# GpSimd's share of the state products, and the places of three background steps, in a kernel of two convolution layers around scans

## The chip, the cores and the metric

The kernel runs on one core of one Trainium2 chip. The metric is the time of one execution on the device in microseconds (us), lower is better; each time is that of the core, as the device reports it. The engines are named as in the profile: PE is the matmul engine (PEld its weight loads), DVE is VectorE, ACT is ScalarE, POOL is GpSimd, SP is the engine whose queue starts the transfers. They run side by side, each takes its own instructions strictly in order, and they wait for each other on semaphores.

## What is computed

The input is 8 images of 64 channels and 128 by 128 pixels, in float32. Layer 0 is a filter whose 9 taps differ from pixel to pixel; layer 1 holds two blocks of a two-way state scan (a "mamba"), between norms and convolutions. Cut to what matters here:

```python
# layer 0: per pixel 9 weights, from two convolutions and a softmax
w_hp = delta - softmax(conv1x1(leaky(conv3x3(x))))
x1 = x + sum(shifted(x, k) * w_hp[:, k] for k in range(9))
# layer 1
x_norm = layernorm(x1)                 # first norm; also feeds the branch dw1
seq = res = layernorm(x_norm)          # second norm
for l in range(2):                     # two blocks
    xz = in_proj(rmsnorm(seq))         # third norm, for block 0
    seq = seq + out_proj(scan_forward(xz) + scan_backward(xz))
# one scan, for each channel d of 128 and state n of 16, along 16384 pixels:
#   h[t] = exp(dt[t] * A[d, n]) * h[t-1] + dt[t] * u[t] * B[n, t]
#   y[t] = sum over n of h[t] * C[n, t]  + D[d] * u[t], then times silu(z)
x2 = x1 + dwconv(dw1(x_norm)) * (conv3x3(rmsnorm(seq)) + res)     # "mix"
out = x2 + ffn(layernorm(x2))          # convolutions, gelu, gate
```

## The kernel before

The whole program is one list of steps. `at(time, phase, fn)` puts a function at a time (a whole number) and at one of seven phases within it, in the order FEED, SCAN, MID, PROD, EXP, DECAY, REST. At the end the list is sorted by time and phase and its functions are called one after the other, so that each engine's queue holds its instructions in just this order. A time has no duration of its own: one unit of it is one scan on VectorE and what was put beside it.

**Scans.** An image has 16,384 pixels, which a pass takes in 16 chunks of T = 1024. A chunk's states (128 channels x 16) are 16 units of 128 partitions x 1024 pixels, two units to a pair. For each image there are four passes (two blocks, two directions): 1 and 3 are "first" passes, which leave their y in DRAM (yf_dram), and 2 and 4 are "second" passes (self.second), which add it in, multiply by the gate and project. So there are 8 x 4 x 16 = 512 chunks and 8192 scans, 1024 of them for an image. For unit u of a chunk that begins at time t0 = b, `Chunk.plan` sets:

- `drive(k)` at b + 2k - 5: bu = dup x bp for a pair, 128x2048 on GpSimd, into one of 4 buffers (L1186).
- `decay(u)` at b + u - 2: w = exp(dt A) on ScalarE, into one of two PSUM tiles (L1194).
- `scan(u)` at b + u on VectorE (L1213 or L1215, by direction). Where the product will be GpSimd's, the scan writes to hs in SBUF, otherwise in place over w.
- `product(u)`: hs x cp, 128x1024, either on VectorE in the same step (L1230) or on GpSimd a step later (L1232, L1234). `on_pool(u)` says which: before the change units 0, 2, 6, 8, 10 and 14 of every chunk, without those a step behind a gelu of the FFN.
- `keep(u)`: ScalarE copies the last state for the next chunk (L1237).
- `collect(k)` at b + 2k + 3 (pairs 0 and 4 a step later): PE sums a pair's products over the states into the one PSUM tile y (L1252). Pairs 0 and 4 first put D u into it (L1245), which needs the tile free.
- `y_out(h)` for the two halves h of a chunk takes y out: on VectorE with the gate in second passes (L1267), on ScalarE as a copy in first passes (L1269), and then `store_y` sends it to DRAM.
- `dtx` makes du for the next chunk, 128x1024 on GpSimd (L1142); `load_hn` loads a chunk's input two chunks ahead.

**Background.** Beside the scans run three other kinds of work. The *front* of the next image (layer 0 and the norms, 16 chunks, one each 24 steps) runs beside the end of pass 3 and most of pass 4; for image 0 half of it runs before the scans (`plan_alone`) and half beside pass 1. The *mix* of an image (16 chunks, one each 13 steps) runs beside the end of its pass 4 and pass 1 of the next image, the *FFN* (16 chunks, one each 24 steps) beside passes 1 to 3 of the next image. For the last image both follow at other paces, and the FFN comes behind the last scan.

In the front, at a chunk's own time a: nine taps, each with `weight(k)` (PE spreads tap k's weights over the channels into the PSUM tile of the tag "bg", L594), `weighted(k)` (VectorE multiplies them with the shifted image, L598) and `gather(k)` (PE adds it into another PSUM tile, L609). The bank "bg" is one buffer: whoever wants it next waits until the last reader is done. The logits, the transposed softmax, and the means and factors of the first and the third norm use it as well. A norm is: a square on ScalarE, `means` (4 small matmuls on PE, L491), `means_out` (ScalarE: Ln, Exp, L497 and L498), `spread` (PE, L504), and a multiplication on VectorE (L629, L661). ScalarE's copies of small tiles, the squares and the images in work take their room from one pool "tmp" of 11 buffers.

Of the kernel before, what the change touches and what calls it, by code (L numbers as in the profile page):

```python
# [21 lines left out]
NCH = HALF // ROWS  # L22
# [14 lines left out]
FEED, SCAN, MID, PROD, EXP, DECAY, REST = range(7)  # L37
# [18 lines left out]
def kernel(ctx: ExitStack, tc: tile.TileContext, a: dict, out: bass.AP):  # L56
# [385 lines left out]
    def tmp(name):  # L442
        return wk.tile([P, N], F32, tag="tmp", name=name, bufs=11)
# [73 lines left out]
    class Front:  # L517
# [131 lines left out]
                )  # L649

        def second_norm(self):
            self.h0, self.sq = self.hc, tmp("sq")
            nc.scalar.activation(self.h0, self.h0, AF.Identity, bias=vec["pe_norm_b"], scale=vec["pe_norm_w"])
            nc.scalar.activation(self.sq, self.h0, AF.Square)

        def store_h(self):
# [11 lines left out]
        def plan(self, a):  # L668
            n1, n2, n3 = self.n1, self.n2, self.n3
            b = a - FRONT_STEP  # L670
            at(b - 5, REST, self.load_xa)
            for i in range(3):
                at(b + 1 + i, REST, self.hidden, i)
            at(b + 5, DECAY, self.hidden_out)
            at(b + 21, REST, self.logits)
            at(b + 23, DECAY, self.less_max)
            at(b + 23, DECAY, self.exps)
            at(b + 25, MID, self.sums)
            at(b + 25, REST, self.softmax)
            for i in range(3):  # L680
                at(b + 26 + 2 * i, DECAY, self.piece, i)
                if i < 2:
                    at(b + 27 + 2 * i, REST, self.less_piece, i)
            at(b + 31, REST, self.turn)
            at(b + 32, DECAY, self.turned)
            at(a + 6, REST, self.load_xb)
            for k in range(9):

                t = a + k + (k >= 3)
                at(t + 11, DECAY, self.weight, k)  # L690
                at(t + 12, MID, self.weighted, k)
                at(t + 13, REST, self.gather, k)
            at(a + 23, DECAY, self.filtered)
            at(a + 23, REST, self.store_x1)
            at(a + 23, REST, self.centered, acc_tile, "x1")
            at(a + 24, DECAY, self.centered_out)
            at(a + 25, REST, lambda: n1.means(bg_tile, self.sq))
            at(a + 26, DECAY, n1.means_out)
            at(a + 27, REST, n1.spread, bg_tile)
            at(a + 29, MID, self.scaled, n1)  # L700
            at(a + 29, DECAY, self.first_norm)
            at(a + 30, REST, self.pointwise)
            at(a + 31, DECAY, self.pointwise_out)
            at(a + 31, REST, self.store_rows, dw_img[self.p], "dwt")
            at(a + 31, REST, self.centered, acc_tile, "xn")
            at(a + 32, DECAY, self.centered_out)
            at(a + 33, REST, lambda: n2.means(acc_tile, self.sq))
            at(a + 34, DECAY, n2.means_out)
            at(a + 35, REST, n2.spread, acc_tile)
            at(a + 37, MID, self.scaled, n2)  # L710
            at(a + 37, DECAY, self.second_norm)
            at(a + 37, REST, self.store_h)
            at(a + 38, REST, lambda: n3.means(bg_tile, self.sq))
            at(a + 39, DECAY, n3.means_out)
            end = a + (49 if self.c < NCH - 1 else 43)
            at(end - 2, REST, n3.spread, bg_tile)
            at(end, MID, self.third_norm)
            at(end, REST, self.store_hn)

        def plan_alone(self, a):  # L720
            n1, n2, n3 = self.n1, self.n2, self.n3
            b = a - FRONT_STEP
            self.alone = True
            one = bg_tile if self.c in (ALONE - 3, ALONE - 1) else mm_tile
            at(b - 5, REST, self.load_xa)
            for i in range(3):
                at(b + 1 + i, REST, self.hidden, i)
            at(b + 5, DECAY, self.hidden_out)
            at(b + 12, REST, self.logits)
            at(b + 14, DECAY, self.less_max)  # L730
            at(b + 14, DECAY, self.exps)
            at(b + 16, MID, self.sums)
            at(b + 16, REST, self.softmax)
            for i in range(3):
                at(b + 17 + 2 * i, DECAY, self.piece, i)
                if i < 2:
                    at(b + 18 + 2 * i, REST, self.less_piece, i)
            at(b + 22, REST, self.turn)
            at(b + 23, DECAY, self.turned)
            at(a + 6, REST, self.load_xb)  # L740
            for k in range(9):

                t = a + k + (k >= 3)
                at(t + 11, DECAY, self.weight, k)
                at(t + 12, MID, self.weighted, k)
                at(t + 13, REST, self.gather, k)
            at(a + 23, REST, self.store_x1)
            at(a + 23, REST, self.centered, one, "x1")
            at(a + 24, DECAY, self.centered_out)
            at(a + 25, REST, lambda: n1.means(one, self.sq))  # L750
            at(a + 26, DECAY, n1.means_out)
            at(a + 27, REST, n1.spread, one)
            at(a + 29, MID, self.scaled, n1)
            at(a + 29, DECAY, self.first_norm)
            bank = y_tile if a + 37 < 3 else acc_tile
            at(a + 30, REST, self.pointwise, bank)
            at(a + 31, DECAY, self.pointwise_out)
            at(a + 31, REST, self.store_rows, dw_img[self.p], "dwt")
            at(a + 31, REST, self.centered, bank, "xn")
            at(a + 32, DECAY, self.centered_out)  # L760
            at(a + 33, REST, lambda: n2.means(bank, self.sq))
            at(a + 34, DECAY, n2.means_out)
            at(a + 35, REST, n2.spread, bank)
            at(a + 37, MID, self.scaled, n2)
            at(a + 37, DECAY, self.second_norm)
            at(a + 37, REST, self.store_h)
            at(a + 38, REST, lambda: n3.means(bg_tile, self.sq))
            at(a + 39, DECAY, n3.means_out)
            end = a + (43 if self.c < ALONE - 1 else 49)
            at(end - 2, REST, n3.spread, bg_tile)  # L770
            at(end, MID, self.third_norm)
            at(end, REST, self.store_hn)
# [12 lines left out]
    class Mix(Front):  # L785
# [40 lines left out]
        def plan(self, a):  # L826
            n1 = self.n1
            for h in range(2):
                at(a - 6 + h, REST, self.load_conv, dw_img[self.p], "dww", h)
                at(a - 4 + h, REST, self.load_conv, xm_img, "xmw", h)  # L830
            at(a - 1, REST, self.load_h)
            for i in range(3):
                at(a + i, REST, self.conv, 0, "dww", i)
                at(a + 3 + i, REST, self.conv, 1, "xmw", i)
            at(a + 3, DECAY, self.branch_out)
            at(a + 2, REST, self.load_x1)
            at(a + 5, REST, self.add_h)
            at(a + 8, MID, self.times)
            at(a + 8, REST, self.plus)
            at(a + 10, REST, self.store_x2)  # L840
            at(a + 10, REST, self.centered, bg_tile, "x1")
            at(a + 11, DECAY, self.centered_out)
            at(a + 12, REST, lambda: n1.means(bg_tile, self.sq))
            at(a + 13, DECAY, n1.means_out)
            at(a + 14, REST, n1.spread, bg_tile)
            at(a + 16, MID, self.scaled, n1)
            at(a + 16, DECAY, self.norm)
            at(a + 16, REST, self.store_rows, xn_img, "hc")

    def plan_mix(b, a, step):  # L850
        at(a - 4, REST, load_weights, 1)
# [176 lines left out]
    class Chunk:  # L1028
# [143 lines left out]
        def on_pool(self, u):  # L1172


            if u % 2 or u % 8 == 4 or self.t0 + u - 1 in gelu_times:
                return False
            return True

        def over_pair(self, what, k):
            j = self.pairs[k][0]  # L1180
# [132 lines left out]
        def plan(self):  # L1313
# [5 lines left out]
                else:  # L1319
                    at(t - 1, REST, fn, *args)  # L1320

            at(b + 3, REST, self.load_hn)
            for h in range(2):
                feed(b + 7 + h, self.conv, h)
                at(b + 7 + h, DECAY, self.conv_out, h)
# [34 lines left out]
            for h in range(2):  # L1360
                if self.second:
                    at(b + 8 * h + 1, REST, self.load_yf, h)
                    at(b + 8 * h + 6, REST, self.add_yf)
                    at(b + 8 * h + 7, REST, self.load_gate, h)
                if self.second:
                    at(b + 8 * h + 11, MID, self.y_out, h)
                else:
                    at(b + 8 * h + 11, DECAY, self.y_out, h)
                    at(b + 8 * h + 12, REST, self.store_y, h)
            if not self.second:  # L1370
                return
            b += U
# [62 lines left out]
```

## Time and profile before

| | |
|---|---|
| time, median of 3 runs | 28,580.81 us (28,557.65 to 28,581.72) |
| the profiled execution | 28,567.34 us |
| its span, first to last instruction | 28,565.6 us |
| from the first to the last scan | 383 us to 28,119 us |
| ScalarE's Exp for the scans (L1194) | 8192 x 1.119 us |
| scans on VectorE (four groups) | 8192 x 2.343 us |
| products on GpSimd (L1232, L1234) | 1515 x 2.409 us, 1445 x 2.374 us |
| taps of the filter on VectorE (L598) | 1152 x 0.673 us |
| transfers | 237 GB/s over the span |

A line of the costliest groups reads: line, engine, operation, what is written and what is read, their shapes, the count, then busy time in us and the mean of one in ns, then the idle time of the engine just ahead of these instructions and who ended most of it. Lines of the timeline begin with start and duration in us, and end with the idle time before and what ended it, in brackets. Lines of the waits give who waited for whom, the total in us, the number of times and the longest. Spans on GpSimd are rough.

### The profile page before, as it was taken

The numbers are of one execution on the slowest core, as the hardware profiler recorded it, in microseconds if no ns is written. First come the engines' busy times: TensorE is split into PE (matmuls) and PEld (weight loads), VectorE is DVE, ScalarE is ACT, GpSimd is POOL, SyncE is SP. The second block draws the span as 40 slices with busy tenths as digits, with TensorE's granted clock in tenths as the row PEclk, the third lists the DMA queues.
The fourth block names the chain that finished last, engine by engine and source line by source line (L and its number), as shares of the span: only waits on it lengthen the run. The fifth ranks groups of instructions, "written<-read, shape, count | busy, mean of one in ns | idle before, by whom it ended". The sixth has DMA issues, their size and how long they took to land. (4 is left out here: it accounts for less than half of the span.)

```text
span 28565.6 us, 310777 instructions
## 1 busy us (share of the span) xinstructions
PE 22791.3 (80%) x97708; PEld 7199.5 (25%) x97708; DVE 27008.8 (95%) x17438; ACT 18796.6 (66%) x29130; POOL 26723.7 (94%) x8092
## 2 busy tenths in 40 slices
PE   7666878878888787887878788787887878878578
PEld 3212322223222232222322222222222222222123
DVE  6999999999999999999999999999999999999997
ACT  4666666666666666666666666666666666666663
POOL 4999999999999999999999999999999999999993
PEclk7778889988899888988889889898898988889789
DMA  5777787777877778777787777777777777777674
GB/s 161 231 241 226 234 258 245 243 227 236 261 246 243 228 235 265 243 240 228 242 256 244 240 230 244 253 246 235 230 251 247 249 229 236 250 245 248 209 256 138
DMA packets 2592494, 6762.73 MB, mean 237 GB/s; under 512 B 431494, under 2 KB 737046, under 8 KB 2589686
## 3 DMA queue, kind: packets, MB, share of 16 engines
q1 hardware_dynamic: 2589958, 6742.69, 73.0%
q8 instruction: 773, 12.66, 0.2%
q14 instruction: 883, 7.23, 0.1%
q10 hardware_dynamic: 880, 0.14, 0.0%
HBM read 5509.49 MB, written 1265.19 MB: 237 GB/s over the span
## 5 line engine op out<-in xcount | busy, mean ns | idle before, releaser
L1186 POOL TENSOR_TENSOR bu<-dup,bp 128x2048 f32<-128x2048 f32 x4096 | 18669.5, 4569 | 30.2 <-DMA hn_dram<-hn 11.4
L1194 ACT ACTIVATE w<-dtp,a_neg 128x1024 f32<-128x1024 f32 x8192 | 9162.7, 1119 | 1498.3 <-DVE hs L1215 661.3
L1230 DVE TENSOR_TENSOR hs<-w,cp 128x1024 f32<-128x1024 f32 x5232 | 6394.1, 1222 | 254.3 <-DMA cp<-bc_dram 72.7
L1215 DVE TENSOR_TENSOR_SCAN w<-w,state,bu 128x1024 f32<-128x1024 f32 x2651 | 6212.2, 2343 | 144.3 <-ACT w L1194 116.8
L1213 DVE TENSOR_TENSOR_SCAN w<-w,state,bu 128x1024 f32<-128x1024 f32 x2581 | 6048.3, 2343 | 136.5 <-ACT w L1194 127.4
L1252 PE MATMUL y<-hs,sel_y 128*32 128x512 f32 x32768 | 4927.9, 681 | 357.4 <-POOL hs L1234 234.8
L1237 ACT COPY state<-w 128x1 f32<-128x1 f32 x5232 | 829.1, 158 | 5461.1 <-DVE hs L1230 5390.7
L1232 POOL TENSOR_TENSOR hs<-hs,cp 128x1024 f32<-128x1024 f32 x1515 | 3649.2, 2409 | 408.9 <-DVE hs L1213 212.3
L1234 POOL TENSOR_TENSOR hs<-hs,cp 128x1024 f32<-128x1024 f32 x1445 | 3430.0, 2374 | 442.3 <-DVE hs L1215 314.6
L1213 DVE TENSOR_TENSOR_SCAN hs<-w,state,bu 128x1024 f32<-128x1024 f32 x1515 | 3550.7, 2344 | 128.0 <-ACT state L1237 76.6
L1215 DVE TENSOR_TENSOR_SCAN hs<-w,state,bu 128x1024 f32<-128x1024 f32 x1445 | 3384.7, 2342 | 105.8 <-ACT state L1237 72.6
L1061 PE MATMUL xp<-hn,wx 128*128 128x512 f32 x4096 | 2353.2, 703 | 908.8 <-ACT xc L1067 397.5
L1245 PE MATMUL y<-xc,dskip 128*64 128x512 f32 x4096 | 1453.6, 796 | 1231.1 <-ACT yv L1269 1083.8
L892 PE MATMUL fp<-fw,bgw 128*128 128x512 f32 (+1 forms) x5760 | 2155.7, 617 | 169.1 <-DMA fw<-xn_dram 162.1
L1103 PE MATMUL dp<-xc,wdt 128*128 128x512 f32 x2048 | 1296.8, 719 | 650.4 <-ACT dt L1110 316.5
L1252 PEld LDWEIGHTS y<-hs,sel_y 128*32 128x32 f32 x32768 | 719.9, 114 | 3866.9 <-issue 2449.9
L68 ACT ACT_TABLE_LOAD x1137 | 1458.8, 1283 | 21.0 <-PEq L1424 0.7
L1067 ACT ACTIVATE xc<-xp,cbias 128x512 f32<-128x512 f32 x1024 | 701.1, 685 | 1156.1 <-PE xp L1061 1152.7
L898 PE MATMUL fp<-fw,bgw 64*128 64x512 f32 (+1 forms) x5760 | 1386.4, 608 | 0.0
L1061 PEld LDWEIGHTS xp<-hn,wx 128*128 128x128 f32 x4096 | 802.2, 214 | 2307.1 <-issue 878.7
L609 PE MATMUL acc<-t,ident 128*128 128x512 f32 x2160 | 1332.1, 705 | 0.7 <-DVE t L598 0.7
L1142 POOL TENSOR_TENSOR du<-dt,xc 128x1024 f32<-128x1024 f32 x512 | 1225.7, 2394 | 42.0 <-ACT dt L1116 42.0
(212 smaller groups left out, 25302.5 us busy)
## 6 DMA issues: line engine op xcount, KB each, us to landing
bp<-bc_dram SPq DMA_DIRECT2D x4096, 256.0 KB, 4.0
dup<-du_dram SPq DMA_DIRECT2D x4096, 256.0 KB, 5.2
dtp<-dt_dram SPq DMA_DIRECT2D x4096, 256.0 KB, 5.1
cp<-bc_dram SPq DMA_DIRECT2D x4096, 256.0 KB, 4.7
hn<-hn_dram SPq DMA_DIRECT2D x1024, 256.5 KB, 4.5
dt_dram<-dt SPq DMA_DIRECT2D x512, 512.0 KB, 2.9
du_dram<-du SPq DMA_DIRECT2D x512, 512.0 KB, 2.6
yf_dram<-yv SPq DMA_DIRECT2D x512, 256.0 KB, 4.3
```

Of the source, the lines that this page charges most:

```text
L68: nc.scalar.preload_act_table_set("natural_log_exp_and_others")
L892: nc.tensor.matmul(o, wpair[:, i, g, m], self.win[h][:, i : i + ROWS, 0:W], start=(i == 0), stop=False)
L1061: nc.tensor.matmul(self.xp[h], wx[:, self.l, self.d, i, :], self.hn2[:, s.start + 2 * i : s.stop + 2 * i], start=(i == 0), stop=(i == 1),)
L1186: nc.gpsimd.tensor_tensor(bu, self.dup[self.pairs[k][1]], self.over_pair("bp", k), ALU.mult)
L1194: nc.scalar.activation(w, self.dtp[gp][:, i, :], AF.Exp, scale=a_neg[:, self.l, self.d, g, j : j + 1])
L1213: nc.vector.tensor_tensor_scan(to, w, bu, s0, ALU.mult, ALU.add)
L1215: nc.vector.tensor_tensor_scan(to[:, ::-1], w[:, ::-1], bu[:, ::-1], s0, ALU.mult, ALU.add)
L1230: nc.vector.tensor_tensor(out, hs, c, ALU.mult)
L1232: nc.gpsimd.tensor_tensor(out, hs, c, ALU.mult)
L1234: nc.gpsimd.tensor_tensor(out[:, ::-1], hs[:, ::-1], c[:, ::-1], ALU.mult)
L1245: nc.tensor.matmul(self.y[C * h : C * h + C, :], dskip[:, self.l, self.d, C * gp : C * gp + C], self.xc[:, s], start=True, stop=False,)
L1252: nc.tensor.matmul(self.y[lo : lo + 32, :], sel_y, hs[:, i, s], start=False, stop=(k % 4 == 3))
```

## The change

It has these parts.

1. `on_pool`: only unit 4 is left out of the even units, and unit 12 in second passes. In first passes GpSimd also makes the product of unit 12, and VectorE no longer does.
2. The front's third norm: its square is taken out of `second_norm` into a function of its own, `third_square`. For chunks 0 to 14 of a front that runs beside scans it is put at a + 46, its mean at a + 47 (before: a + 38) and Ln and Exp at a + 48; the third norm and its store come at a + 55 instead of a + 49. The last chunk and the fronts of `plan_alone` keep their times. The filter's taps, which had a free step ahead of tap 3, now follow each other without one.
3. In first passes `y_out` and `store_y` come one step sooner.
4. The mix's second half (`centered` to the store of xn) comes one step later.
5. `load_hn` of chunk 14 of all 512 comes two steps later.

```diff
@@ second_norm @@
-            self.h0, self.sq = self.hc, tmp("sq")
+            self.h0 = self.hc
             nc.scalar.activation(self.h0, self.h0, AF.Identity, bias=vec["pe_norm_b"], scale=vec["pe_norm_w"])
+
+        def third_square(self):
+            self.sq = tmp("sq")
             nc.scalar.activation(self.sq, self.h0, AF.Square)
@@ Front.plan @@
-                t = a + k + (k >= 3)
+                t = a + k
                 at(t + 11, DECAY, self.weight, k)
                 at(t + 12, MID, self.weighted, k)
                 at(t + 13, REST, self.gather, k)
...
-            at(a + 38, REST, lambda: n3.means(bg_tile, self.sq))
-            at(a + 39, DECAY, n3.means_out)
-            end = a + (49 if self.c < NCH - 1 else 43)
+            late, end = (a + 46, a + 55) if self.c < NCH - 1 else (a + 37, a + 43)
+            at(late, DECAY, self.third_square)
+            at(late + 1, REST, lambda: n3.means(bg_tile, self.sq))
+            at(late + 2, DECAY, n3.means_out)
             at(end - 2, REST, n3.spread, bg_tile)
             at(end, MID, self.third_norm)
             at(end, REST, self.store_hn)
@@ plan_alone @@
+            at(a + 37, DECAY, self.third_square)
@@ Mix.plan @@
-            at(a + 10, REST, self.centered, bg_tile, "x1")
-            at(a + 11, DECAY, self.centered_out)
...
+            at(a + 11, REST, self.centered, bg_tile, "x1")
+            at(a + 12, DECAY, self.centered_out)
...
@@ Chunk.on_pool @@
-            if u % 2 or u % 8 == 4 or self.t0 + u - 1 in gelu_times:
+            if u % 2 or u == 4 or self.t0 + u - 1 in gelu_times:
                 return False
-            return True
+            return u != 12 or not self.second
@@ Chunk.plan @@
-            at(b + 3, REST, self.load_hn)
+            at(b + (5 if self.i == NCH - 2 else 3), REST, self.load_hn)
...
-                    at(b + 8 * h + 11, DECAY, self.y_out, h)
-                    at(b + 8 * h + 12, REST, self.store_y, h)
+                    at(b + 8 * h + 10, DECAY, self.y_out, h)
+                    at(b + 8 * h + 11, REST, self.store_y, h)
```

More of the change, by code (lines that the diff above doesn't have):

```diff
@@ L840, in plan @@
             at(a + 10, REST, self.store_x2)
[L841 to L848 removed]
+            at(a + 11, REST, self.centered, bg_tile, "x1")
+            at(a + 12, DECAY, self.centered_out)
+            at(a + 13, REST, lambda: n1.means(bg_tile, self.sq))
+            at(a + 14, DECAY, n1.means_out)
+            at(a + 15, REST, n1.spread, bg_tile)
+            at(a + 17, MID, self.scaled, n1)
+            at(a + 17, DECAY, self.norm)
+            at(a + 17, REST, self.store_rows, xn_img, "hc")
     def plan_mix(b, a, step):
```

## The prediction

> **What bounds the kernel now.** I read the page first: the shares of the engines and the costliest groups.
>
> ```profile
> PE 22791.3 (80%) x97708; PEld 7199.5 (25%) x97708; DVE 27008.8 (95%) x17438; ACT 18796.6 (66%) x29130; POOL 26723.7 (94%) x8092
> ...
> L1186 POOL TENSOR_TENSOR bu<-dup,bp 128x2048 f32<-128x2048 f32 x4096 | 18669.5, 4569 | 30.2 <-DMA hn_dram<-hn 11.4
> L1230 DVE TENSOR_TENSOR hs<-w,cp 128x1024 f32<-128x1024 f32 x5232 | 6394.1, 1222 | 254.3 <-DMA cp<-bc_dram 72.7
> ```
>
> VectorE and GpSimd stand at 95% and 94%, too close to say which sets the end. So I cut the trace where a pass begins, at the scan of unit 0 of every sixteenth chunk, and asked for the engines' busy time by pass. The first four rows are passes 1 to 4 of image 4; then pass 1 of image 0, pass 3 of image 0, pass 3 of image 7. The columns are the stretch, its length, and busy time with the count of instructions for PE, PEld, DVE, ACT and POOL; then clock and DMA.
>
> ```profile
> 14294.40:15139.70 845.30, 659.75 (x2842) 178.70 (x2840) 802.78 (x461) 559.05 (x840) 844.28 (x252) 0.89 0.78 253
> 15139.70:16000.10 860.40, 757.11 (x3154) 234.92 (x3150) 832.40 (x506) 592.27 (x880) 812.27 (x230) 0.96 0.74 246
> 16000.10:16858.60 858.50, 648.00 (x2750) 201.03 (x2749) 832.90 (x542) 573.16 (x900) 836.30 (x263) 0.84 0.72 228
> 16858.60:17772.60 914.00, 762.36 (x3535) 274.72 (x3533) 869.66 (x609) 624.06 (x1020) 843.36 (x267) 0.90 0.75 242
> 383.20:1257.00 873.80, 640.22 (x2655) 208.47 (x2654) 837.05 (x545) 574.25 (x915) 835.17 (x262) 0.78 0.70 224
> 2091.00:2956.10 865.10, 602.67 (x2536) 182.22 (x2535) 827.57 (x534) 561.41 (x882) 846.85 (x267) 0.80 0.71 225
> 26438.10:27260.60 822.50, 470.19 (x1684) 103.61 (x1682) 784.83 (x428) 516.55 (x748) 820.07 (x237) 0.73 0.62 209
> ```
>
> In pass 1 GpSimd is busy for 844.3 of 845.3 us while VectorE idles 42.5 us: GpSimd sets the time there. In pass 3 it idles 22 us, in pass 2 48 us, in pass 4 71 us. Then I looked at GpSimd's queue inside pass 1.
>
> ```profile
> 14715.90 4.79 POOL L1186 TENSOR_TENSOR bu<-dup,bp 128x2048 f32<-128x2048 f32 x1
> 14720.39 2.61 POOL L1232 TENSOR_TENSOR hs<-hs,cp 128x1024 f32<-128x1024 f32 x1
> 14722.71 4.76 POOL L1186 TENSOR_TENSOR bu<-dup,bp 128x2048 f32<-128x2048 f32 x1
> 14727.19 2.60 POOL L1232 TENSOR_TENSOR hs<-hs,cp 128x1024 f32<-128x1024 f32 x1
> 14729.50 4.76 POOL L1186 TENSOR_TENSOR bu<-dup,bp 128x2048 f32<-128x2048 f32 x1
> ```
>
> The recorded durations overlap: a product that "takes" 2.61 us is followed 2.32 us later. What a back-to-back instruction costs is the distance of starts: 4.49 and 4.48 us for a drive, 2.32 and 2.31 us for a product. One more reading from the timeline: drives and pairs of scans stand in one order, so the lead of GpSimd (end of a drive to the start of the scan that reads it) can be followed. In image 4 its minimum per chunk falls from 6.7 us in chunk 0 of pass 1 to 0.0 in chunk 3, stays at 0 to 0.5 us up to chunk 9 and is back at 7.4 us in chunk 15; pass 3 starts at 7.2 and ends at 10.2 us. So GpSimd has a cushion of some 7 us, and no more. Last, what VectorE waits for in pass 4, and the longest wait but one:
>
> ```profile
> DVE t L598 <- PE wb L594: 21.7, 13, 3.1
> DVE hs L1213 <- ACT state L1237: 7.2, 10, 1.0
> DVE hn L661 <- PE rb L504: 4.8, 5, 1.6
> ```
> ```profile
> 17410.13 0.69 ACT L1067 ACTIVATE xc<-xp,cbias 128x512 f32<-128x512 f32 x1 [2.73 <-PE xp L1061]
> 17410.71 0.26 ACT L497 ACTIVATE r<-ms,eps 128x8 f32<-128x8 f32 x1
> 17411.03 0.38 PE L594 MATMUL wb<-wt,sel_k 65*128 65x512 bf16 x1 [0.94 <-ACT r L497]
> 17411.44 0.69 DVE L598 TENSOR_TENSOR t<-xb,wb 128x512 f32<-128x512 f32 x1 [2.95 <-PE wb L594]
> ```
>
> The third norm's mean and the filter's weights use one PSUM bank. ScalarE must take the mean out (L497), but it stands behind the conv eviction L1067, which waited 2.73 us for PE; then tap 3's weight, and VectorE has waited 2.95 us. Of the 21.7 us, 16.5 us are at tap 3, right behind the mean, and 5.2 us at tap 8.
>
> **Part 1: unit 12 on GpSimd.** Its product leaves VectorE in all 256 chunks of first passes (1 and 3): 256 x 1.222 = 313 us off VectorE, 19.6 us a pass. On GpSimd it costs 16 x 2.31 = 37.0 us a pass, 591 us in all. In the built order the products on GpSimd go from 2960 to 3216. What a pass becomes is GpSimd's busy time before, plus 37.0, corrected for the change in lead:
> - Pass 1, images 1 to 7 (before 844.4 to 846.0 us): 844 + 37 = 881. The lead used to come back to 7 by the end; now it stays at 0, and pass 2, with 48 us of GpSimd idle, restores it: 881 - 7 = 874, so +29, times 7 = +203. Bounds +26 (a lead of 10 drawn down) to +36 (none drawn): 182 to 252.
> - Pass 3, images 1 to 6 (mean 857.3): 836.3 + 37.0 = 873.3, less the 3 by which the lead grew, less 4 as it now falls from 7 to 3 = 866, so +9, times 6 = +54. Bounds +6 (lead to 0) to +37 (the 22 us of idle stays): 36 to 222.
> - Pass 3, image 7: 820.1 + 37.0 against 822.5, lead to 0 in both: +35 (33 to 37).
> - Image 0: pass 1, 835.2 + 37.0 less some 1 for the lead = 871 against 873.8; I take 0 (-3 to 20). Pass 3, 846.9 + 37.0 less 9 of growth plus 2 = 877: +12 (8 to 37).
>
> Sum: 203 + 54 + 35 + 0 + 12 = **+304 us** (256 to 568). The 313 us off VectorE bring nothing where GpSimd is last, and are in the sum already where it isn't.
>
> The Trainium skill, "Perfetto Trace Analysis", section Identifying the Most-Contended Engine, says that the engine with the highest occupancy is the bottleneck, and that it may change between regimes. By its first half over the whole span, VectorE (95%) is to be relieved, and the sum would be -313 for this part and 28,135 us in all; by its second half, read pass by pass, it agrees with the rows.
>
> **Part 2: the mean behind the filter, without the free step at tap 3.** Nothing is added: 1 square, 4 small matmuls, Ln and Exp per chunk of the front, later; the two stores of hn go 6 steps later on SP. It acts where VectorE is last: pass 4, images 0 to 6 (913.9 to 917.2 us). In pass 3 and in image 0's pass 1 the same waits are hidden by GpSimd. The tap-3 wait goes: 16.5 us an image. What is late next: the mean, now at front step 23, stands between the logits' readers and the next chunk's first mean in the same bank, each a step (3.3 to 3.6 us) apart; and tap 8, now a step sooner. I take 17 an image, **-119 us** for seven. Bounds: 0 (as long a wait moves elsewhere) to 27 an image (the rb waits of 4.8 too): 0 to -189. A loss can't be excluded: h0 keeps one of the 11 tmp buffers 6 steps longer.
>
> **Part 3: at nothing.** y_out stands a scan sooner in first passes: PE's wait for yv (PEld y from L1245, 47.6 us in pass 1 of image 4, 89.0 in pass 3) shrinks, but GpSimd hides it. On ScalarE it now stands ahead of unit 13's Exp instead of unit 14's; if PE is late, that Exp is late, and the scan. VectorE's slack of 42.5 + 19.6 us in pass 1 covers this. In pass 3, 25.6 + 19.6 - 9 covers less; gone, it is in the +37 bound. The store of y moves with it, same count. The mix's centered goes a step later: PE waited 46.0 us in pass 1 for POOL's x (PEld cp), hidden by GpSimd. load_hn moves in one chunk of 512 (its two transfers land after 4.5 us, two steps are some 6.6). The tail after the last scan (446 us) keeps its order but for the last mix chunks: 0.
>
> **Sum.** The profiled run took 28,567.3 us (span 28,565.6): 28,567.3 + 304 - 119 = 28,752. The median of the runs is 13.5 us above it, so I forecast **28,765 us**, 0.65% slower.
>
> **Rivals.**
> - The tap-3 wait only changes place (PE at 762 of 914 us in pass 4 is often late, and its queue order decides): 28,765 + 119 = 28,885. For it: the chain begins with PE's xp, which stays. Against: the Ln leaves the chain. 20%.
> - No cushion: the waits that make GpSimd idle in pass 3 stay and each product costs its 2.31 us in full: 28,581 + 591 - 119 = 29,053. For it: a late product on GpSimd holds PE's collect and everything behind. Against: in pass 1 GpSimd idles 1 us with the lead at 0, so lateness of the others doesn't reach it. 7%.
> - More gain: the low end of part 1 and all waits of part 2: 28,581 + 256 - 189 = 28,648. 10%.
> - Faster: GpSimd's records are rough, and its 100% in pass 1 is room that isn't seen; VectorE sets the time everywhere and gets its 313 us back: 28,581 - 313 - 119 = 28,149. It decides if 16 chunks with one product more still fit into 845 us, which needs GpSimd 4.2% quicker per instruction (881/845). For it: VectorE's 95%. Against: starts 2.31 and 4.48 us apart, a lead of 0, and VectorE idle in the same stretch. 3%.
>
> **How the numbers follow.** The forecast's own case has 60%, and reaches from 28,680 to 28,860. The range of 28,630 to 28,930 takes in the first rival and most of the third, and leaves out the second and the last and part of the edges. About 0.2% (57 us) is what a measurement of this kernel can tell from no change. Faster than that 3%, within it 5% (the far end of the third rival), slower 92%.
>
> **What will show it.** Pass 1 of images 1 to 7 near 874 us with GpSimd idle under 3 us, its lead at 0 from chunk 3 or sooner to the end, and VectorE idle up from 42 to some 90 us. Pass 3 near 866 us. Pass 4 near 897 us with hardly a wait of L598's line behind tap 3. Pass 2 unchanged near 860 us. I am wrong if pass 1 stays near 845 us, if pass 2 grows by what is left over from pass 1, or if the filter's wait turns up at another tap.

## The result and the profile after

The changed kernel takes 28,852.8 us (median of 4 runs, 28,841.6 to 28,867.4) against 28,581.3 us for the kernel before in the same session: a ratio of 1.0097, 95% interval 1.0079 to 1.0114. It is slower by 272 us, where 184 us were forecast. The page of the profiled execution, its line of the engines and the groups that answer to those shown of before:

```profile
span 28839.8 us, 310478 instructions
...
PE 23007.1 (80%) x97708; PEld 7256.9 (25%) x97708; DVE 26736.7 (93%) x17182; ACT 18781.5 (65%) x29130; POOL 27301.0 (95%) x8348
...
L1191 POOL TENSOR_TENSOR bu<-dup,bp 128x2048 f32<-128x2048 f32 x4096 | 18706.9, 4573 | 30.4 <-DMA hn_dram<-hn 11.4
...
L1235 DVE TENSOR_TENSOR hs<-w,cp 128x1024 f32<-128x1024 f32 x4976 | 6079.9, 1222 | 261.3 <-DMA cp<-bc_dram 120.5
...
L1218 DVE TENSOR_TENSOR_SCAN hs<-w,state,bu 128x1024 f32<-128x1024 f32 x1643 | 3852.6, 2345 | 429.8 <-POOL bu L1191 204.6
```

VectorE does 256 products fewer and is busy for 272 us less, not for the 313 us that their recorded durations add up to; GpSimd has become the fuller engine. In the last line a small wait has grown: forward scans that write to hs wait for GpSimd's drives for 204.6 us in all, where it was 11.7 us. The same cut by pass shows where. The rows are passes 1 to 4 of image 4, with the columns of the table in the prediction:

```profile
14415.10:15285.10 870.00, 670.39 (x2822) 180.82 (x2820) 786.55 (x445) 559.59 (x837) 870.00 (x265) 0.86 0.75 244
15285.10:16150.20 865.10, 764.37 (x3174) 236.97 (x3170) 832.70 (x506) 593.10 (x881) 821.95 (x233) 0.96 0.74 248
16150.20:17019.50 869.30, 655.05 (x2750) 205.03 (x2749) 814.39 (x526) 571.69 (x900) 867.32 (x276) 0.84 0.70 225
17019.50:17924.00 904.50, 766.73 (x3535) 276.50 (x3533) 869.97 (x609) 622.06 (x1020) 848.66 (x270) 0.89 0.75 244
```

In pass 1 GpSimd has no idle time left (870.00 of 870.00 us); VectorE's idle time there went from 42.5 to 83.4 us. Within the pass GpSimd does 13 instructions more (265 against 252), not 16, so some of its work has moved behind the end of the pass. Pass 3 has turned into a stretch of the same kind: GpSimd idles 2 us where it idled 22. Pass 2, in which no product was moved, is longer too (860.4 to 865.1 us). Pass 4 is shorter, 914.0 to 904.5 us.

Set against the terms of the forecast, the span's growth of 274 us comes apart like this (the sums over the images, from the same cut):

| stretch | forecast | measured |
|---|---|---|
| pass 1, images 1 to 7 | +203 | +174 |
| pass 1, image 0 | 0 | 0 |
| pass 2, all images | 0 | **+69** |
| pass 3, images 1 to 6 | +54 | +68 |
| pass 3, image 7 | +35 | +32 |
| pass 3, image 0 | +12 | +12 |
| pass 4, images 0 to 6 | -119 | **-73** |
| pass 4 of image 7, and ahead of and behind the scans | 0 | -7 |
| sum | +185 | +274 |

What VectorE waits for in pass 1 of image 4 (who waited for whom, total us, times, longest): the lines of the drives before, then those after, and then the list for pass 4 after:

```profile
DVE hs L1213 <- POOL bu L1186: 1.6, 2, 0.9
DVE w L1213 <- POOL bu L1186: 1.2, 2, 0.9
```
```profile
DVE hs L1218 <- POOL bu L1191: 28.5, 32, 2.2
...
DVE w L1218 <- POOL bu L1191: 7.5, 9, 2.1
```
```profile
DVE hs L1218 <- ACT state L1242: 7.1, 9, 1.2
DVE hs L1218 <- ACT w L1199: 7.1, 5, 1.9
DVE mx L554 <- PE lp L548: 4.9, 4, 1.7
DVE t L598 <- PE wb L594: 4.5, 6, 1.0
DVE w L1218 <- ACT w L1199: 3.6, 6, 0.8
```

In pass 1 VectorE now waits 36 us for drives, where it was 2.8 us. In pass 4 the filter's wait on its weights fell from 21.7 to 4.5 us, as the prediction had it, but the list is longer than it was: the logits (mx, 4.9 us) were no wait before, and the waits for the Exp of the scans (the two lines that end in "ACT w") went from 5.8 to 10.7 us. One of these, from the timeline of pass 4:

```profile
17507.43 0.69 ACT L1072 ACTIVATE xc<-xp,cbias 128x512 f32<-128x512 f32 x1 [5.30 <-PE xp L1066]
17508.01 0.62 ACT L657 ACTIVATE sq<-hc 128x512 f32<-128x512 f32 x1
17508.53 1.11 ACT L1199 ACTIVATE w<-dtp,a_neg 128x1024 f32<-128x1024 f32 x1
17509.75 2.35 DVE L1218 TENSOR_TENSOR_SCAN hs<-w,state,bu 128x1024 f32<-128x1024 f32 x1 [1.87 <-ACT w L1199]
```

PE is late with the conv's xp, ScalarE waits 5.30 us for it with everything behind it held, the moved square of the third norm (L657) comes next, and only then the Exp, for which VectorE has waited 1.87 us.

### The profile page after: what moved, and what is told of

Read it like the earlier page. It is cut to its first block, busy times and chain, and to the rows that moved or that the text cites. A ratio compares the mean times of both kernels' runs of the same rounds, so it can differ in the third digit from the quotient of the medians.

```text
span 28839.8 us, 310478 instructions
## 1 busy us (share of the span) xinstructions
PE 23007.1 (80%) x97708; PEld 7256.9 (25%) x97708; DVE 26736.7 (93%) x17182; ACT 18781.5 (65%) x29130; POOL 27301.0 (95%) x8348
## 5 line engine op out<-in xcount | busy, mean ns | idle before, releaser
L1257 PE MATMUL y<-hs,sel_y 128*32 128x512 f32 x32768 | 5063.1, 699 | 1587.8 <-POOL hs L1237 806.9
L1235 DVE TENSOR_TENSOR hs<-w,cp 128x1024 f32<-128x1024 f32 x4976 | 6079.9, 1222 | 261.3 <-DMA cp<-bc_dram 120.5
L1220 DVE TENSOR_TENSOR_SCAN w<-w,state,bu 128x1024 f32<-128x1024 f32 x2523 | 5910.1, 2342 | 162.1 <-ACT w L1199 119.7
L1218 DVE TENSOR_TENSOR_SCAN w<-w,state,bu 128x1024 f32<-128x1024 f32 x2453 | 5746.2, 2343 | 143.7 <-ACT w L1199 72.4
L1218 DVE TENSOR_TENSOR_SCAN hs<-w,state,bu 128x1024 f32<-128x1024 f32 x1643 | 3852.6, 2345 | 429.8 <-POOL bu L1191 204.6
L1237 POOL TENSOR_TENSOR hs<-hs,cp 128x1024 f32<-128x1024 f32 x1643 | 3956.1, 2408 | 268.3 <-DVE hs L1218 166.3
L1239 POOL TENSOR_TENSOR hs<-hs,cp 128x1024 f32<-128x1024 f32 x1573 | 3752.2, 2385 | 327.4 <-DVE hs L1220 250.4
L1220 DVE TENSOR_TENSOR_SCAN hs<-w,state,bu 128x1024 f32<-128x1024 f32 x1573 | 3685.7, 2343 | 387.0 <-ACT state L1242 235.8
L1066 PE MATMUL xp<-hn,wx 128*128 128x512 f32 x4096 | 2422.1, 721 | 799.1 <-ACT sq L1299 325.0
L897 PE MATMUL fp<-fw,bgw 128*128 128x512 f32 (+1 forms) x5760 | 2217.0, 630 | 242.0 <-DMA fw<-xn_dram 234.9
L1108 PE MATMUL dp<-xc,wdt 128*128 128x512 f32 x2048 | 1357.4, 750 | 526.3 <-ACT dt L1115 193.8
L1250 PE MATMUL y<-xc,dskip 128*64 128x512 f32 x4096 | 1385.6, 761 | 317.8 <-ACT yv L1274 214.1
```

The source lines that it names most:

```text
L897: nc.tensor.matmul(o, wpair[:, i, g, m], self.win[h][:, i : i + ROWS, 0:W], start=(i == 0), stop=False)
L1066: nc.tensor.matmul(self.xp[h], wx[:, self.l, self.d, i, :], self.hn2[:, s.start + 2 * i : s.stop + 2 * i], start=(i == 0), stop=(i == 1),)
L1218: nc.vector.tensor_tensor_scan(to, w, bu, s0, ALU.mult, ALU.add)
L1220: nc.vector.tensor_tensor_scan(to[:, ::-1], w[:, ::-1], bu[:, ::-1], s0, ALU.mult, ALU.add)
L1235: nc.vector.tensor_tensor(out, hs, c, ALU.mult)
L1237: nc.gpsimd.tensor_tensor(out, hs, c, ALU.mult)
```

## The experiments

The experiments ran in later sessions, in which the kernel before took 28,598 to 28,616 us. Each ratio is taken against that kernel in its own session, and microseconds that are set beside a ratio are worked out from it. Lengths of passes are taken from the traces and compared with the trace of the kernel before from the first session. That is good to about 1 us in some places (pass 3 of image 7 takes 821.8 to 822.8 us in all eight later traces that leave its products alone) and not in others: ahead of the first scan the later traces take 389 to 398 us against 383, and pass 2 differs by up to 12 us an image in kernels that leave it alone.

**1 and 2. The parts by themselves.** First the kernel before with part 1 alone, then the changed kernel without part 1.

```diff
@@ the kernel before: part 1 alone @@
-            if u % 2 or u % 8 == 4 or self.t0 + u - 1 in gelu_times:
+            if u % 2 or u == 4 or self.t0 + u - 1 in gelu_times:
                 return False
-            return True
+            return u != 12 or not self.second
@@ the changed kernel: parts 2 to 5 alone @@
-            if u % 2 or u == 4 or self.t0 + u - 1 in gelu_times:
+            if u % 2 or u % 8 == 4 or self.t0 + u - 1 in gelu_times:
                 return False
-            return u != 12 or not self.second
+            return True
```

> The kernel before with part 1 alone (unit 12's product on GpSimd in first passes). Theory: GpSimd's queue sets the first passes, so this part alone costs what passes 1 to 3 grew by in the changed kernel, 174 + 69 + 111 = 354 us less the 0 to 20 us that the other parts may have given back: 28,900 to 28,950, ratio 1.011 to 1.013, with pass 1 near 870 us and the first chunks of pass 2 longer by some 8 us. Rival: the new places (y_out sooner ahead of unit 13's Exp, the mix later) make up much of the loss, and part 1 alone costs under 250 us, ratio under 1.009.

> The changed kernel with the products' places of the kernel before (parts 2 to 5 alone). Theory: only pass 4 changes, by the 78 us that it lost in the changed kernel, and passes 1 to 3 are within 5 us an image of before: 28,490 to 28,510, ratio 0.9970 to 0.9980. Rival: the new places cost time in first passes, and this is at or above the kernel before, ratio 1.000 or more.

Part 1 alone: 28,958.8 us, ratio 1.0124 (1.0109 to 1.0139), some 354 us (the medians differ by 347). Parts 2 to 5 alone: 28,482.0 us, ratio 0.9955 (0.9940 to 0.9970), some 129 us the other way. So the loss is part 1's, and the rest is a gain; it is larger than the 70 to 90 us expected: besides pass 4 (77 us in images 0 to 6), pass 1 is shorter by 29 us in all eight images and pass 3 by 21, while pass 2 is longer by 17. The two add up to +225 us against +277 measured together. Each interval is some 43 us wide to either side, so whether the parts disturb each other stays open. Pass 1 of image 4 with part 1 alone, and the pass 2 behind it:

```profile
14483.80:15354.60 870.80, 667.27 (x2823) 180.20 (x2822) 786.62 (x445) 556.82 (x836) 870.78 (x265) 0.87 0.75 242
15354.60:16222.90 868.30, 766.37 (x3171) 237.26 (x3169) 832.90 (x507) 593.09 (x881) 821.07 (x233) 0.95 0.74 247
```

The 870 us of pass 1 are there without any of the other parts, in all seven images (870.3 to 871.6). Pass 2 is longer by 46 us in all, against 69 in the changed kernel.

**3. y_out back at its old step**, in the changed kernel:

```diff
-                    at(b + 8 * h + 10, DECAY, self.y_out, h)
-                    at(b + 8 * h + 11, REST, self.store_y, h)
+                    at(b + 8 * h + 11, DECAY, self.y_out, h)
+                    at(b + 8 * h + 12, REST, self.store_y, h)
```

> The changed kernel with y_out and store_y of first passes at their old step. Theory: GpSimd hides y_out, so nothing changes by more than 20 us: 28,830 to 28,875, ratio to before 1.009 to 1.0105. Rival: y_out ahead of unit 13's Exp makes scans late, and this is faster than the changed kernel by 50 us or more, ratio under 1.008.

28,868.5 us, ratio 1.0093 (1.0076 to 1.0110): no difference from the changed kernel that can be told. In the sum y_out's place is worth nothing that this run can show, in either direction.

**4. What makes pass 2 longer.** The last 4 chunks of each first pass were given back to VectorE.

```diff
-            return u != 12 or not self.second
+            return u != 12 or not (self.second or self.i % NT >= NT - 4)
```

> The changed kernel, but in the last 4 chunks of each first pass unit 12's product is back on VectorE, so that GpSimd regains its lead before the next pass begins. Theory: the growth of the first two chunks of pass 2 (5 to 9 us an image, 61 us in seven images) comes from GpSimd's late start into it; here it is gone, and pass 1 is shorter by up to 5 us as well: 28,750 to 28,800, ratio 1.006 to 1.0077. Rival: pass 2 grows for another reason (the places of other work); then only the products taken away count where GpSimd binds, at most 4 x 2.31 us in a pass, the first chunks of pass 2 stay as long as in the changed kernel, and the time is 28,800 to 28,850.

28,792.5 us, ratio 1.0065 (1.0050 to 1.0080), in the range of the theory. But in the first four chunks of pass 2 the growth is halved (31 us for 61, images 1 to 7), not gone, and part of the lead is still lost. Put beside the other kernels, the time of the first two chunks goes with the size of the lead (means over images 1 to 7; the lead is the smallest distance from the end of a drive to the scan that reads it, in the last chunk of pass 1):

| kernel | lead at the end of pass 1, us | first two chunks of pass 2, us |
|---|---|---|
| before | 7.4 | 105.4 |
| part 2 alone (experiment 6) | 7.2 | 106.7 |
| parts 2 to 5, square early (experiment 7) | 6.6 | 107.1 |
| parts 2 to 5 alone | 5.7 | 106.1 |
| changed, not in the last 4 chunks | 2.8 | 108.6 |
| changed, y_out at its old step | 0.8 | 112.2 |
| part 1 alone | 0.6 | 111.7 |
| changed | 0.3 | 113.7 |
| changed, second dose (experiment 5) | 0.0 | 113.5 |

The lead is not the whole of it. Within one kernel these chunks stand at about 105 us in some images and at about 108.5 in others, with a lead of some 7 us in both. And image 0, beside whose passes no FFN runs, entered pass 2 with a lead of 0.4 us in the kernel before, and its first two chunks took 104.7 us.

GpSimd does have idle time in pass 2, but it gets it late: with the lead at 0, products are late, PE is held at their sums, and ScalarE and VectorE behind PE. The timeline of the changed kernel at the start of pass 2 of image 4:

```profile
15284.78 2.48 POOL L1237 TENSOR_TENSOR hs<-hs,cp 128x1024 f32<-128x1024 f32 x1
...
15286.38 0.69 ACT L1115 ACTIVATE dt<-dp,dtb 128x512 f32<-128x512 f32 x1 [3.81 <-PE dp L1108]
...
15288.30 2.36 DVE L1220 TENSOR_TENSOR_SCAN w<-w,state,bu 128x1024 f32<-128x1024 f32 x1 [0.87 <-ACT w L1199]
...
15294.13 1.06 PE L1257 MATMUL y<-hs,sel_y 128*32 128x512 f32 x8 [1.10 <-POOL hs L1237]
```

A product of pass 1 still runs when pass 2 has begun (in the kernel before, the last one had ended 1.1 us ahead of it); ScalarE waits 3.81 us for PE, the Exp behind it is late, and the second scan of the pass waits for it.

There is a second way, over the queue of the transfers. The store of du can start only when GpSimd has made du, and in the trace nothing is issued on that queue from 15,301.8 us until that store starts at 15,314.6; the load of the gate follows it at 15,321.6. The queue's wait for du in the first two chunks of pass 2 of image 4, before and after, and VectorE's wait for the gate, of which the kernel before has none there:

```profile
SPq L1146 <- POOL du L1142: 9.1, 2, 5.0
```
```profile
SPq L1151 <- POOL du L1147: 18.4, 2, 12.7
```
```profile
15327.00 0.69 DVE L1272 TENSOR_TENSOR yv<-y,gate 128x512 f32<-128x512 f32 x1 [3.31 <-DMA gate<-gate_dram]
```

Over these two chunks of images 1 to 7, VectorE's idle time went from 10.7 to 66.2 us: 34.5 us of it are waits for the Exp and 15.1 for the gate, neither of which was there before, and only 2.8 are waits for drives. PE's waits for GpSimd's products went from 0 to 17.8 us, those for the FFN's input, a transfer too, from 18.9 to 42.2. How much each of the two ways costs was not tested.

**5. A second dose.** Unit 4 on GpSimd as well, in first passes of the changed kernel.

```diff
-            if u % 2 or u == 4 or self.t0 + u - 1 in gelu_times:
+            if u % 2 or self.t0 + u - 1 in gelu_times:
                 return False
-            return u != 12 or not self.second
+            return u not in (4, 12) or not self.second
```

> The changed kernel with unit 4's product on GpSimd in first passes as well: 256 products more, a second dose. Theory: GpSimd already idles 0 to 2 us in first passes and its lead is used up, so nothing hides these, and each costs its 2.31 us: some 570 to 590 us above the changed kernel, ratio to before 1.029 to 1.031; pass 1 near 907 us, pass 3 near 906 us. Rival: what the first dose cost per product (347 us / 256 = 1.36 us) is what a product costs, as VectorE gives a part back: about 350 us more, ratio 1.022.

29,471.5 us, ratio 1.0305 (1.0290 to 1.0320): 0.0208 of 28,581 above the changed kernel, some 595 us for 256 products, 2.32 us each. That is the distance of starts that the prediction read from the timeline, and the rival (350 us, with VectorE giving a part back) is out. The two intervals leave some 65 us to either side, though, 0.25 us a product, so the total can't tell 2.31 us from the recorded duration of 2.41. The rows can. Pass 1 of image 4:

```profile
14721.60:15628.00 906.40, 679.50 (x2824) 182.00 (x2822) 770.16 (x428) 558.55 (x836) 906.40 (x281) 0.85 0.73 234
```

Pass 1 grew by 36.4 us for 16 products (36.3 to 36.6 in images 1 to 7), 2.28 us each. Sixteen distances of 2.31 us make 37.0; sixteen of the durations that are recorded in this pass of the changed kernel, 2.43 us on average, would make 38.9. The first dose cost 354 us by itself, 1.38 us a product, because it still found idle time in pass 3 and a lead to use up.

**6. Part 2 alone**, on the kernel before. It needs the later load_hn (part 5): image 0's front then stores a chunk of hn at step 196, and that chunk was read at step 195.

```diff
-                t = a + k + (k >= 3)
+                t = a + k
...
-            at(a + 38, REST, lambda: n3.means(bg_tile, self.sq))
-            at(a + 39, DECAY, n3.means_out)
-            end = a + (49 if self.c < NCH - 1 else 43)
+            late, end = (a + 46, a + 55) if self.c < NCH - 1 else (a + 37, a + 43)
+            at(late, DECAY, self.third_square)
+            at(late + 1, REST, lambda: n3.means(bg_tile, self.sq))
+            at(late + 2, DECAY, n3.means_out)
...
-            at(b + 3, REST, self.load_hn)
+            at(b + (5 if self.i == NCH - 2 else 3), REST, self.load_hn)
```

> The kernel before with part 2 alone (the third norm's mean behind the filter, the taps without a free step) and the later load_hn of one chunk, which the later store of the third norm needs. Theory: the whole gain of the parts other than part 1 is in pass 4, 70 to 85 us, ratio 0.9970 to 0.9976; passes 1 and 3 of images 1 to 7 stay within 2 us. Rival: part 2 also shortens the first passes (as the run of parts 2 to 5 did by 3 us in pass 1 and 3 to 5 us in pass 3), ratio 0.9955 or less; then y_out and the mix's step are worth nothing.

28,448.9 us, ratio 0.9947 (0.9932 to 0.9962): as good as parts 2 to 5 together. Both expectations are half right: pass 1 of images 1 to 7 did stay within 2 us, but image 0's pass 1 (-17 us) and pass 3 (-1 to -8 us in images 0 to 6), where the front stands beside scans as well, gained too. So the y_out and mix steps are not shown to bring anything in the sum, and part 2 accounts for the whole gain within what the intervals tell. By the rows the other steps move time about: pass 4 of images 0 to 6 takes 901.6 us on average with part 2 alone and 904.3 with parts 2 to 5, pass 1 of images 1 to 7 845.6 and 842.1. The 2.7 us of pass 4 go with the mix's step: with that step kept and y_out put back (experiment 3), pass 4 takes 904.1 us.

**7. The square back in its old step**, with parts 2 to 5:

```diff
-            at(late, DECAY, self.third_square)
+            at(a + 37, DECAY, self.third_square)
```

> Parts 2 to 5 with the third norm's square back in its old step, a + 37, and only its mean behind the filter. Theory: in pass 4 the square at a + 46 stands in ScalarE's queue between a late conv eviction and the Exp of a scan, and VectorE's waits of 1.0 to 1.9 us at front step 1 (four an image) come from it; they shrink by 0.6 us each, so pass 4 is 2 to 4 us shorter than without this, 15 to 30 us in all: ratio 0.9945 to 0.9955. Rival: the late conv eviction alone makes the wait, and nothing changes in pass 4 (under 1 us an image).

28,508.8 us, ratio 0.9967 (0.9954 to 0.9980): outside both expectations, and rather worse. Pass 4 takes 904.5 to 904.7 us in three images and 908 to 912 in the four others before the last. So the square ahead of the Exp is not what costs there. That PE's late xp is what costs, as the timeline of pass 4 suggests, was not tested by itself.

**8. Unit 12 where GpSimd has idle time.** In second passes instead of first ones, with parts 2 to 5.

```diff
-            return u != 12 or not self.second
+            return u != 12 or (self.second and (self.b < B - 1 if self.l else self.b > 0))
```

> The products' places of before in first passes, but unit 12 on GpSimd in second passes (not in pass 2 of image 0, nor in pass 4 of image 7), with parts 2 to 5 of the change. Theory: there GpSimd idles 40 to 61 us a pass with a lead of 7 to 10 us, and VectorE sets the time; 37.0 us fit in, and VectorE's 19.6 us count where GpSimd's 849 to 880 us allow: pass 2 from 860 to about 850 us, pass 4 from 905 to about 886 us, so 100 to 200 us below the kernel without this: 28,280 to 28,400, ratio 0.989 to 0.993. Rival: a product on GpSimd costs time wherever it is put, since it comes a step later and holds PE's sum: ratio 0.996 or more.

28,429.4 us, ratio 0.9941 (0.9924 to 0.9957), only some 40 us below the kernel without it, which the intervals can't tell from nothing: a miss. Pass 4 of image 4 without it (parts 2 to 5 alone), then pass 4 and pass 2 with it:

```profile
16798.70:17703.50 904.80, 766.91 (x3535) 276.55 (x3533) 870.07 (x609) 622.07 (x1020) 843.81 (x267) 0.89 0.76 243
```
```profile
16790.30:17694.90 904.60, 768.04 (x3535) 277.76 (x3533) 851.43 (x593) 620.67 (x1020) 880.11 (x283) 0.88 0.76 243
15082.60:15935.00 852.40, 756.43 (x3154) 236.73 (x3150) 812.67 (x491) 591.15 (x880) 849.01 (x247) 0.96 0.74 249
```

Pass 2 is what was expected, 852 us with GpSimd nearly full. Pass 4 did not move: VectorE is busy for 18.6 us less than without (851.43 against 870.07) and takes 904.6 us all the same. The longest of its waits in that pass:

```profile
DVE hs L1218 <- ACT state L1242: 19.3, 14, 2.3
```

It was 7.1 us without unit 12 on GpSimd, and all of it falls on the scan of unit 14: ScalarE is late there, behind the silu of step 11, and VectorE, relieved two units earlier, arrives sooner and waits 12.2 us longer at this place alone. So two more runs, on part 2 alone: unit 12 on GpSimd in pass 2 (images 1 to 7), and beside that unit 4 in pass 4 (images 0 to 6).

```diff
@@ unit 12 in pass 2 @@
-            if u % 2 or u % 8 == 4 or self.t0 + u - 1 in gelu_times:
+            if u % 2 or u == 4 or self.t0 + u - 1 in gelu_times:
                 return False
-            return True
+            return u != 12 or (self.second and self.l == 0 and self.b > 0)
@@ and unit 4 in pass 4 @@
-            if u % 2 or u == 4 or self.t0 + u - 1 in gelu_times:
+            if u % 2 or self.t0 + u - 1 in gelu_times:
                 return False
+            if u == 4:
+                return self.second and self.l == 1 and self.b < B - 1
```

> Part 2 alone (ratio 0.9947) and unit 12 on GpSimd in pass 2 of images 1 to 7. Theory: in pass 2 GpSimd's 49 us of idle take the 37.0 us, and 7 to 10 us a pass are gained, as where unit 12 was on GpSimd in all second passes: 50 to 70 us in all, ratio 0.9922 to 0.9932. Rival: the gain seen there was the scatter of pass 2 from image to image; ratio 0.9945 or more.

> As the first of these three, and in pass 4 of images 0 to 6 unit 4 (not 12) on GpSimd. Theory: unit 12 brought nothing in pass 4 because VectorE then only waits longer at unit 14 for ScalarE, which is late from the silu (that wait went from 7.1 to 19.3 us); ahead of unit 4's neighbours VectorE waits for nobody, so here 8 to 18 us a pass come off, 55 to 125 us in all, ratio 0.988 to 0.991. Rival: in pass 4 PE's queue sets the pace, wherever VectorE is relieved: pass 4 stays within 3 us of 902 us, ratio as the first of these three.

With pass 2: 28,378.4 us, ratio 0.9918 (0.9902 to 0.9935), a little more than was expected; pass 2 of images 1 to 7 takes 850.9 us on average, against 862.8 with part 2 alone. With unit 4 in pass 4 too: 28,335.8 us, ratio 0.9902 (0.9887 to 0.9917), and pass 4 is shorter by 9.6 to 14.6 us an image than in the run before it (901.9 us on average). Image 4:

```profile
16725.50:17617.00 891.50, 764.26 (x3517) 278.12 (x3515) 850.04 (x593) 619.33 (x1017) 874.97 (x281) 0.89 0.76 246
```

A product of the same size in the same pass, 8 units sooner, is worth 10 to 15 us, where that of unit 12 was worth nothing. (Of the distance from 904.6 to 891.5 us some 3 us are the mix's step, which only the first of the two kernels has.) The pass 1 behind it pays 4 to 7 us of that back: the lead at the end of pass 4 is down from 6 to 7 us to 0 to 2, as it was at the end of pass 1 in experiment 4.

**9. Less on GpSimd in pass 1.** On top of the first of these two, unit 8 on VectorE in chunks 4 to 11 of pass 1, images 1 to 7.

```diff
+            if u == 8 and not self.second and self.l == 0 and self.b > 0 and 4 <= self.i % NT < 12:
+                return False
```

> The same, and unit 8's product taken off GpSimd in chunks 4 to 11 of pass 1 of images 1 to 7, where GpSimd's lead is 0. Theory: GpSimd sets the time there in the kernel before already, so 8 x 2.31 = 18.5 us less on it shorten pass 1 until VectorE (1.22 us a chunk more) takes over: 5 to 15 us a pass, 35 to 100 us in all, ratio 0.989 to 0.992. Rival: VectorE takes over at once, and pass 1 is no shorter, or longer by up to 10 us: ratio 0.9925 or more.

28,330.6 us, ratio 0.9899 (0.9884 to 0.9914). Pass 1 of image 4:

```profile
14179.00:15013.90 834.90, 656.11 (x2842) 178.32 (x2840) 811.42 (x469) 559.52 (x840) 825.89 (x244) 0.90 0.81 256
```

Taking 8 products off GpSimd makes pass 1 about 10 us shorter (8 to 11 in images 1 to 7) although VectorE does them in its place: the opposite of the change, in the pass where the change hurt most.

**10. All of it**: part 2, unit 12 in pass 2, unit 4 in pass 4, unit 8 in pass 1.

```diff
-            if u % 2 or u % 8 == 4 or self.t0 + u - 1 in gelu_times:
+            if u % 2 or self.t0 + u - 1 in gelu_times:
                 return False
-            return True
+            if u == 4:
+                return self.second and self.l == 1 and self.b < B - 1
+            if u == 8 and not self.second and self.l == 0 and self.b > 0 and 4 <= self.i % NT < 12:
+                return False
+            return u != 12 or (self.second and self.l == 0 and self.b > 0)
```

> Part 2, unit 12 on GpSimd in pass 2, unit 4 in pass 4, unit 8 back on VectorE in chunks 4 to 11 of pass 1. Theory: the three places add up, 0.9899 for the one with pass 1 relieved, less 0.0016 for unit 4 in pass 4; and as pass 1 now has room, the 3 to 8 us that unit 4 in pass 4 cost at the start of pass 1 (28 us in all) are partly absorbed: ratio 0.9865 to 0.989, about 28,200 to 28,270. Rival: the gains share one slack, and the ratio stays at 0.9895 or more.

28,265.6 us, ratio 0.9885 (0.9868 to 0.9901): 1.15% under the kernel before, and faster than both kernels. The gains add up as expected, but the interval still takes in the rival's 0.9895; and what unit 4 costs at the start of pass 1 is not absorbed (839.7 us on average, against 835.1 in experiment 9).

## Why the prediction was right

The measured time lies inside the range, 88 us above the forecast. The causes were mostly right, but the closeness is partly luck, since errors of both signs met: pass 2 came out 69 us too long and pass 4 gained 46 us too little, while pass 1 cost 29 us less than was forecast.

- **What bounds what.** Right. Pass 1 is GpSimd's: it grows with a product more in each chunk (experiment 1) and with two more (experiment 5), and shrinks with one less in half of the chunks (experiment 9); what is taken off VectorE brings nothing there. The rule of the fuller engine over the whole span would have had this change gain. (Of the two things that the prediction says of that rule, the one on regimes stands in the page's next section, Optimization Strategy.)
- **The price of a product, 2.31 us by the distance of starts.** Right: pass 1 grew by 2.28 us a product in the second dose, where the durations recorded there would have made 2.43. The Trainium skill, "Perfetto Trace Analysis", section GPSIMD Engine Instruction, says to time GpSimd by the spacing of starts and not by the reported spans; the rows of that run bear it out.
- **The lead as a cushion that is used up once.** Right in kind, but reckoned too small for pass 1: +24.8 us on average where 37.0 were added, forecast +29 with a lower bound of +26. By the counts of the rows, three of GpSimd's instructions more than before fell behind the end of the pass. In pass 3 +11 came where +9 was forecast, but that is luck in part: with part 1 alone, and in the changed kernel with y_out at its old step, pass 3 of images 1 to 6 grew by 93 and 90 us and not by 68.
- **"Pass 2, with 48 us of GpSimd idle, restores it."** This step failed, by a sign that the prediction itself had named ("if pass 2 grows by what is left over from pass 1"), and it is the larger part of what was missing: pass 2 grew by 69 us in all where 0 stood, 61 us of it in the first 4 chunks of images 1 to 7. The lead is made good within two or three chunks, but at VectorE's expense, over PE and ScalarE and over the queue of the transfers (experiment 4). Not all of the 69 us need be the lead: in the two kernels with parts 2 to 5 alone and with part 2 alone, pass 2 is 17 and 24 us longer than in the trace of before, with a lead of 5.7 and 7.2 us.
- **Part 2, -17 us an image.** The mechanism was right: the wait at tap 3 went from 16.5 to 0.9 us in image 4, and the wait on the weights fell by 17.2 us in all. The term was too large: pass 4 gained 10.4 us an image on average, 13.6 with part 2 alone. Of what was said to be late next, tap 8 was not (its 5.2 us went too; 3.6 us stand at tap 4). The logits, among whose readers the mean now stands, became a wait of 4.9 us, and ScalarE's Exp (4.9 us more) was not named; VectorE's idle time in pass 4 fell from 44.3 to 34.5 us.
- **"The same waits are hidden by GpSimd" in pass 3 and in image 0's pass 1.** Not so in the kernel before: part 2 alone shortens pass 3 by 1 to 8 us an image and image 0's pass 1 by 17 us (experiment 6), and the prediction's own row for image 0's pass 1 has GpSimd idle for 39 us.
- **Part 3 at nothing.** Right for the sum, by experiments 3 and 6. Pass by pass it was not nothing: the mix's step costs some 3 us in pass 4, which is the difference between the 13.6 and the 10.4 us above.
- The first rival (the tap-3 wait only changes place) had the nearer number, 28,885 us, but not the cause.

## What to carry to other kernels

Where two engines stand within a few per cent of each other, cut the trace by stage before work is moved between them: here the engine that was full in one stage paid each instruction at its full price, and the relief of the other counted for nothing there. A queue that runs ahead is a cushion that can be spent once, and here part of what was spent at the end of a stage was paid for at the start of the next. And relief of an engine only counts if that engine isn't about to wait for a third one: a product moved eight units earlier was worth 10 to 15 us a pass, where the later one had been worth nothing.

## What was not expected of the hardware

GpSimd's recorded durations of the same product are not constant while the distance of starts stays at 2.31 us: in pass 1 of image 4 of the kernel before, a chunk's products are recorded with 2.41 us on average in the first chunk and with 2.70 in the thirteenth, in pass 1 of image 2 of the same run with 2.34 to 2.44. GpSimd's queue runs without a pause through these chunks in both, so that is not by itself the reason, and the reason stays open. So the durations of GpSimd's instructions should not be added up; the union of its records (the time in which at least one of them runs), or the spacing of starts, can be.
